# One-core convolution, attention and expert layer: each chunk's attention sums taken in two parts, and another order of loads at the end

## The chip, the cores and the metric

The kernel runs on one core of a Trainium2 chip: TensorE (PE, matrix products, and PEld, its weight loads), VectorE (DVE), ScalarE (ACT), GpSimd (POOL) and SyncE (SP), whose queue issues all the DMAs here. The metric is the device time of one execution in microseconds, the median of several runs.

## The reference, cut to what matters

Eight images of 128 channels and 36 x 36 = 1296 positions. Layer 0 is a convolution block with attention over 1156 positions and a residual. Layer 1 reads the result as 1296 tokens of 128 channels:

```python
t = _to_tokens(x)
t = t + _L1_attn_ref(_ln_t(t), ...)     # scores: sum_d w_d tanh(q_id + k_jd), softmax over j
t = t + _L1_ffn_ref(_ln_t(t), ...)      # 64 experts, each takes its 8 best tokens
x = _from_tokens(t, x)
```

```python
t = jnp.tanh(q[:, :, None, :] + k[:, None, :, :])
scores = jnp.einsum('bijd,d->bij', t, w) + bw[0]
attn = jax.nn.softmax(scores, axis=-1)
return jnp.einsum('bij,bjd->bid', attn, x)
```

In the expert layer each expert softmaxes its gate logits over the tokens, takes the weighted sum of its eight best tokens (`pooled`), passes it through two matrices with a gelu between, and adds its output back to those tokens with the same weights.

## The kernel before, in words

**The loop.** The work on the scores is divided into 8 batches (images) of 3 chunks of 432 queries, and each chunk goes through 11 tiles of keys: ten of 128 keys and a remainder of 16, which stands sixth in the list `order`. One tile of one chunk is a unit, and a unit takes 12 slots (3 for the remainder): 2952 slots in all. A slot is one turn of the main loop: TensorE makes two products for the denominators (`d`, three slots ahead) and two for the numerators (`n`), both at line L802 (L809 in the remainder unit); ScalarE takes Ln of `d` (L824) and, every second slot, Exp of two such (L827), which gives reciprocals; VectorE multiplies (L849, L855) and GpSimd and VectorE add up (L851, L862). Seven slots after a unit's last, its sum becomes the exponentials `e` of the scores (L887), a tile of 128 keys by 432 queries.

**Other work in the slots.** All the rest is written as generators in four lanes: `first_of_all` (query features of the next chunk), `urgent` (attend), `gates` (gating of the batch before) and `background` (layer 0, tokens and keys of the next batch). In each slot `take_turns` lets each lane take a step without matrix products, and `matmul_turn` lets one lane issue some, held by `PACE` to 370 units of work a slot on the average.

**Attend.** When all 11 `e` tiles of a chunk are there, `attend` goes to the urgent lane. For each of its four pieces of 108 queries (`TPC`) it issues the load of the piece's tokens into `t2` (L619), sums e times xh over the first six tiles into PSUM, copies this to `sums` (L632), sums the other five, adds (L634), divides and adds the tokens (L637), and takes statistics (L641, L642). Tiles `e` lie in a pool of NKT + 1 = 12. The gates lane takes no products while something is urgent. In the last batch, attend goes on to the gate logits of its chunk.

**The tail.** After the last slot the memory of the scoring pools is given back. SP issues, in this order: the expert biases (L1000, L1003), the first token tile of the last attend (`urgent.run`), the weights of four of 16 groups of experts (L992, L994, eight DMAs of 1 MB), then what `drain(*urgent)` issues: the other three token tiles (L619), t2d of the last chunk (L683) and, from `gate_tokens`, gd (L735). Then come eight loads of `gates` (L1025). The loop over the expert groups (inner L1033 and L1037, turned L1046, outer L1058) asks for the weights of one more group with each group that is done. After it: four stores of `out_s` to eod (L1077), eight loads of the residuals `res` from t2d (L1083) into a pool `lasts` of their own, four loads of `eo` (L1086) with an addition each (L1087), and for each batch three products (L1093) with three additions into `res` (L1094), followed by its store to the output (L1095).

All DMAs share eight completion semaphores in turn, so that a DMA waits until the one eight before it has landed. Pools rotate their buffers: a new tile waits for the readers of the one that had its buffer. `big` is a pool of eight tiles of 6 KB a partition, which the loop uses for images, weights of the convolutions, `xh`, `t2`, `probs`, `gt` and others.

Of the kernel before, what the change touches and what calls it, by code (L numbers as in the profile page):

```python
# [9 lines left out]
F32 = mybir.dt.float32  # L10
# [16 lines left out]
REM = KT[-1][1]  # L27
# [5 lines left out]
E, HID, O = 64, 512, 128  # L33
# [31 lines left out]
def kernel(  # L65
# [28 lines left out]
    nc = tc.nc  # L94
    mm = nc.tensor.matmul
# [25 lines left out]
    with ExitStack() as loop, ExitStack() as score:  # L121

        def pool(name, bufs, stack=loop, side="left", space=bass.MemoryType.SB):
            return stack.enter_context(
                tc.tile_pool(name=name, bufs=bufs, side=side, space=space)
            )


        big = pool("big", 8)
        chunks = pool("chunks", 14)  # L130
        etp = pool("etp", NKT + 1)
        one = pool("one", 1)
        two = pool("two", 2)
        kfp = pool("kfp", 3, score, "right")
# [9 lines left out]
        def big_tile(name):  # L144
            return big.tile([128, NT * 128], F32, tag="big", name=name)
# [4 lines left out]
        def aux(name):  # L150
            return ps_n.tile([128, 512], F32, tag="n", name=name)
# [4 lines left out]
        def load_x(b):  # L156
# [27 lines left out]
            out=gavg3, in_=gavg3, compare_op=ALU.is_ge, fill=0.0, base=0,  # L184
# [3 lines left out]
            out=gavg3, in_=gavg3, compare_op=ALU.is_ge, fill=0.0, base=C // G - 1,  # L188
# [46 lines left out]
        def bmm(out, lhsT, rhs, **kw):  # L235
            behind[0] += max(out.free_size(), 128) + 20
            mm(out, lhsT, rhs, **kw)  # L237
# [367 lines left out]

        attended = {}

        def attend(b, c, es):


            xh, _, xr = prepared[b]
            if c == 0:
                t2 = big_tile("t2").rearrange("p (t c) -> p t c", c=128)
                mv = two.tile([T, NT, 2], F32, tag="t2_mv", name="t2_mv")
                attended[b] = (t2, mv)
            t2, mv = attended[b]
            for i in range(TPC):
                at = c * TPC + i
                nc.sync.dma_start(t2[:T, at, :], tokd[b][at * T : (at + 1) * T])  # L619
                sums = two.tile([T, C + 1], F32, tag="sums", name="sums")  # L620
                for some in (range(6), range(6, NKT)):
                    pa = aux("pa1")[:T, : C + 1]
                    for j in some:
                        if j < NKT - 1:
                            e, v = es[j][:, i * T : (i + 1) * T], xh[:, j, :]
                        else:
                            rows = slice(32 * i, 32 * i + REM)
                            e, v = es[j][rows, :T], xr[rows]
                        bmm(pa, e, v, start=(j == some[0]), stop=(j == some[-1]))
                    yield TAKE  # L630
                    if j < NKT - 1:
# [5 lines left out]
                nc.vector.scalar_tensor_tensor(  # L637
                    t2[:T, at, :], pa[:, :C], inv, t2[:T, at, :], ALU.mult, ALU.add
                )
                st = small.tile([T, 6], F32, tag="t2_st", name="t2_st")  # L640
                nc.vector.bn_stats(st, t2[:T, at, :])  # L641
                nc.vector.bn_aggr(mv[:, at, :], st)  # L642
                yield matmuls()
            if c == NCH - 1:
                prepared.pop(b)
            if b == NB - 1:
# [120 lines left out]
        order = list(range(NKT - 1))  # L767
        order.insert(5, NKT - 1)
        units = [(b, c, j) for b in range(NB) for c in range(NCH) for j in order]
        slots = []  # L770
# [105 lines left out]
            nc.gpsimd.tensor_add(d, d, s[:, 0, T : 2 * T])  # L876
            return d

        es = {}

        def exps(p, u, d):
            b, c, j = units[u]

            while urgent and len(es.get((b, c), ())) == 1:
                urgent.run(p)
            e = etp.tile([128, CH], F32, tag="e", name="e")
            nc.scalar.activation(e[:, : d.shape[-1]], d, AF.Exp, bias=eb_s)  # L887
            es.setdefault((b, c), {})[j] = e
# [18 lines left out]
        first_of_all, urgent, gates, background = lanes = [Lane() for _ in range(4)]  # L907
        balance = [0]
# [29 lines left out]
        for u in range(2):  # L938
            prefetch(u)
        for p in range(LAG):  # L940
            denominators(p)
        pending = deque()
        for p, (u, k) in enumerate(slots):
            b, c, j = units[u]
# [44 lines left out]
        def load_experts(g):  # L989
            es = slice(g * EG, (g + 1) * EG)  # L990
            w1 = wts.tile([128, EG, HID], F32, tag="w1", name="w1")
            nc.sync.dma_start(w1, weight1[es, :128, :].rearrange("e d h -> d e h"))  # L992
# [19 lines left out]


    last = ctx.enter_context(tc.tile_pool(name="last", bufs=1))
    lasts = ctx.enter_context(tc.tile_pool(name="lasts", bufs=NB))

    def aux(name):
        return ps_last.tile([128, 512], F32, tag="aux", name=name)

    nc.vector.tensor_copy(pooled_s[:, :, NB - 1], pooled[:, :, NB - 1])  # L1020
    gates = []
    for h in range(NB // 2):
        gates.append(last.tile([128, N], F32, tag=f"gates{h}", name="gates"))
        for b in (2 * h, 2 * h + 1):
            nc.sync.dma_start(gates[h][E * (b % 2) : E * (b % 2) + E], gd[b])  # L1025

    out_s = last.tile([128, NGR, O], F32, tag="out_s", name="out_s")
    hidden, hidden_t, sums_of = {}, {}, {}
# [48 lines left out]
        nc.sync.dma_start(eods[q], out_s[32 * q : 32 * q + NB])  # L1077


    res, eos = [], []  # L1080
    for b in range(NB):
        res.append(lasts.tile([C, N], F32, tag="res", name="res"))
        nc.sync.dma_start(res[b], t2d[b])  # L1083
    for h in range(NB // 2):
        eos.append(last.tile([128, O], F32, tag=f"eo{h}", name="eo"))
        nc.sync.dma_start(eos[h], eod[2 * h : 2 * h + 2].rearrange("b e o -> (b e) o"))  # L1086
        nc.vector.tensor_add(eos[h], eos[h], b2_s)  # L1087
    for b in range(NB):
        half = slice(E * (b % 2), E * (b % 2) + E)
# [5 lines left out]
        nc.sync.dma_start(out[b], res[b])  # L1095


# [60 lines left out]
```

## Time and profile before

| | us |
|---|---|
| median of 3 runs (6334.52 to 6347.67) | 6334.6 |
| the profiled execution, as a run | 6322.6 |
| its span, first to last instruction | 6320.9 |
| Ln of the slots, first and last start | 182.1, 6128.4 |
| last exponential `e` ends | 6137.7 |
| last product of `ppool` ends | 6193.0 |
| `out_s` copied for the last time, from | 6276.5 |

The granted TensorE clock was 0.974 of full speed over the span; in the last 190 us it was at 0.50 to 0.60 in many stretches. "Busy" of an engine is the time in which it had an instruction running; for PE the ends are modelled. A wait in square brackets is idle time of the engine just before the instruction and what ended it. SPq is SP's queue: the duration of a DMA there is that of its issue, not of its transfer.

### The profile page before, as it was taken

To read this page: it belongs to the slowest core of one execution; us is meant where nothing else is said; L and a number is where in the kernel's file an instruction comes from. 1 tells how busy PE (TensorE), PEld (TensorE's weight loads), DVE (VectorE), ACT (ScalarE), POOL (GpSimd) and SP (SyncE) were. 2 spreads that over 40 slices of the span, in tenths; PEclk is the share of its full clock that TensorE was granted. 3 is DMA by queue.
4 is the path that set the end of the run, shared out by engine and by line. 5 is a ranking of instruction groups with operands and counts; after the bars stand their busy time and mean duration, and the time that the engine had idled before them with its cause. 6 is when DMAs were issued, how large, how long until landed. Compare 5 with 4: busy or idle time off the path is not lost.

```text
span 6320.9 us, 107144 instructions
## 1 busy us (share of the span) xinstructions
PE 6067.5 (96%) x40632; PEld 2825.9 (45%) x40632; DVE 4894.6 (77%) x9499; ACT 5360.3 (85%) x5426; POOL 4655.2 (74%) x2782
## 2 busy tenths in 40 slices
PE   8999999999999999999999999999999999999986
PEld 4444454444544444444444444444454444544433
DVE  3687778877788778887788787887778878778862
ACT  1788998888988889889888898888898988999970
POOL 3677777787778877778777786777777777778870
PEclk9999999999999999999999999999999999999997
DMA  0200011100210011100111001100021000100027
GB/s 27 71 30 22 23 64 37 31 24 27 68 36 20 29 35 58 34 27 22 51 44 36 22 23 59 42 30 25 23 69 36 23 25 27 59 28 28 25 69 256
DMA packets 155286, 265.81 MB, mean 42 GB/s; under 512 B 53712, under 2 KB 79824, under 8 KB 154768
## 3 DMA queue, kind: packets, MB, share of 16 engines
q1 hardware_dynamic: 154768, 258.95, 12.8%
q8 instruction: 319, 5.23, 0.4%
q14 instruction: 199, 1.63, 0.1%
HBM read 196.81 MB, written 61.83 MB: 41 GB/s over the span
## 4 chain that ended last, share of the span: by engine, by line
PE 68%; DVE 11%; ACT 8%; issue 7%; POOL 4%; DMA 1%; SPq 1%; POOLq 0%; DVEq 0%; ACTq 0%
PE n L802 31%; PE d L802 10%; PE pc L237 8%; PE pa L237 7%; ACT lq L824 5%; DVE n L849 3%; PE s L237 3%; DVE rp L855 3%; PE pk L237 2%; POOL accp L862 2%; DVE accd L851 2%; PE pq L237 1%; PE n L809 1%; PE d L809 1%; POOL qf L601 1%
## 5 line engine op out<-in xcount | busy, mean ns | idle before, releaser
L862 POOL TENSOR_TENSOR accp<-accp,rp 128x864 f32<-128x864 f32 x1464 | 2965.3, 2026 | 1137.6 <-DVE rp L855 1045.7
L802 PE MATMUL n<-qf,kf 32*128 32x432 f32 (+1 forms) x11520 | 3244.9, 575 | 54.4 <-DVE accd L851 10.0
L824 ACT ACTIVATE lq<-d 128x864 f32<-128x864 f32 x2952 | 2559.8, 883 | 587.2 <-PE d L802 515.1
L802 PE MATMUL d<-qf,kf 32*128 32x432 f32 (+1 forms) x11520 | 2889.0, 564 | 41.4 <-ACT lq L824 37.9
L855 DVE TENSOR_TENSOR rp<-n,lq 128x432 f32<-128x432 f32 x3984 | 2201.6, 600 | 565.5 <-PE d L802 374.4
L827 ACT ACTIVATE lq<-lq 128x1728 f32<-128x1728 f32 x1488 | 2431.1, 1634 | 47.1
L802 PEld LDWEIGHTS n<-qf,kf 32*128 32x128 f32 (+1 forms) x11520 | 1173.4, 185 | 1659.2 <-DVE rp L855 505.7
L802 PEld LDWEIGHTS d<-qf,kf 32*128 32x128 f32 (+1 forms) x11520 | 1036.0, 187 | 405.0 <-issue 236.0
L849 DVE TENSOR_TENSOR n<-n,lq 128x432 f32<-128x432 f32 x1440 | 812.0, 608 | 246.2 <-PE n L802 219.3
L851 DVE TENSOR_TENSOR accd<-n,accd 128x432 f32<-128x432 f32 x1440 | 867.9, 603 | 24.7
L860 POOL TENSOR_TENSOR accp<-rp 128x864 f32<-128x864 f32 x264 | 534.7, 2026 | 145.1 <-DVE rp L855 143.6
L869 POOL TENSOR_TENSOR accp<-accp 128x432 f32<-128x432 f32 x264 | 291.8, 1105 | 17.1
L237 PE MATMUL pa<-xh,e 128*108 128x129 f32 x1920 | 263.7, 284 | 30.4 <-DVE t L637 19.5
L237 PEld LDWEIGHTS pa<-xh,e 128*108 128x108 f32 x1920 | 224.3, 175 | 153.5 <-DVE rp L855 76.4
L872 POOL TENSOR_TENSOR accd<-accp,accd 128x432 f32<-128x432 f32 x240 | 266.0, 1108 | 34.8 <-DVE accd L851 17.2
L601 POOL TENSOR_SCALAR qf<-qf,cs_s 128x432 f32<-128x432 f32 x192 | 261.3, 1367 | 39.1 <-ACT qf L600 39.1
L237 PE MATMUL s<-q,k 128*116 128x432 f32 x480 | 228.8, 568 | 2.6 <-DVE q L260 2.1
L237 PEld LDWEIGHTS pk<-xT,a_k 128*128 128x128 f32 x1408 | 171.9, 193 | 108.6 <-issue 27.5
L381 ACT ACTIVATE e<-s 116x432 f32<-116x432 f32 x240 | 125.4, 522 | 109.7 <-PE s L237 108.6
L374 POOL TENSOR_TENSOR tot<-tot,e 116x432 f32<-116x432 f32 x192 | 212.6, 1107 | 5.1
L237 PE MATMUL pa<-e,vw 116*128 116x432 f32 x480 | 206.2, 556 | 3.9 <-DVE accd L851 3.0
L844 DVE TENSOR_TENSOR accd<-n,lq 128x432 f32<-128x432 f32 x240 | 144.8, 603 | 83.9 <-PE n L802 52.2
(180 smaller groups left out, 4025.0 us busy)
## 6 DMA issues: line engine op xcount, KB each, us to landing
kf<-kd SPq DMA_DIRECT2D x240, 512.0 KB
kd<-ks SPq DMA_DIRECT2D x160, 256.0 KB
w<-in_weight_dram SPq DMA_DIRECT2D x32, 1024.0 KB
x<-in_x_dram SPq DMA_DIRECT2D x8, 648.0 KB
t<-tokd SPq DMA_DIRECT2D x96, 54.0 KB
t2d<-t2T SPq DMA_DIRECT2D x24, 216.0 KB
res<-t2d SPq DMA_DIRECT2D x8, 648.0 KB
out_dram<-res SPq DMA_DIRECT2D x8, 648.0 KB
```

Source lines behind the costliest of these rows:

```text
L237: mm(out, lhsT, rhs, **kw)
L601: nc.gpsimd.tensor_scalar(qf[:, 1, :], qf[:, 0, :], cs_s[:, q : q + 1], None, ALU.mult)
L802: mm(outs[h][:, :CH], kf[rows[h], q, :], qf_of[b, c, q][rows[h], part, :], start=True, stop=True)
L824: nc.scalar.activation(lq[:, o : o + 2, :], d[:, :, :CH], AF.Ln)
L827: nc.scalar.activation(some, some, AF.Exp, scale=-1.0)
L849: mult(ns[h], ns[h], lq[:, o + h, :])
L851: nc.vector.tensor_add(live["d"], ns[h], live["d"])
L855: mult(rp[:, h, :], ns[h], lq[:, o + h, :])
L860: nc.gpsimd.tensor_add(live["p"], live["r"], rp)
L862: nc.gpsimd.tensor_add(live["p"], live["p"], rp)
L869: nc.gpsimd.tensor_add(s[:, 0, :], s[:, 0, :], s[:, 1, :])
L872: nc.gpsimd.tensor_add(d, s[:, 0, :], d)
```

## The change

Attend now enters the urgent lane when six of the chunk's eleven `e` tiles are there (`FIRST`). It first issues all four token loads, takes the first six tiles for all four pieces of queries and keeps the four sums in one tile `sums`; it then waits in its lane until the other five tiles are there, and finishes the four pieces. Tiles `e` lie in a pool of nine (`NES`), counted in `live_es`: when nine are taken, the urgent lane is run until some are given back. Gating waits until the batch's last attend is over (`whole`), and no longer stands back while something is urgent. At the end, SP's queue has the weights of four groups ahead of the biases, with the last token tiles loaded well before. The pool `big` outlives the loop, and the residuals are loaded into its eight buffers, each after one of the gate loads, ahead of the expert loop and of the fifth group's weights. The last products go in pairs, one for each batch of a pair, on the two halves of TensorE's rows; six additions are followed by two stores.

```diff
+FIRST = 6
+NES = 9
-        big = pool("big", 8)
+        big = pool("big", 8, ctx)
-        etp = pool("etp", NKT + 1)
+        etp = pool("etp", NES)
...
+            own = range(c * TPC, (c + 1) * TPC)
+            for at in own:
+                nc.sync.dma_start(t2[:T, at, :], tokd[b][at * T : (at + 1) * T])
+
+            def attended_to(i, some):
+                pa = aux("pa1")[:T, : C + 1]
+                for j in some:
...
+                    bmm(pa, e, v, start=(j == some[0]), stop=(j == some[-1]))
+                return pa
+
+            sums = one.tile([T, TPC, C + 1], F32, tag="sums", name="sums")
             for i in range(TPC):
-                at = c * TPC + i
-                nc.sync.dma_start(t2[:T, at, :], tokd[b][at * T : (at + 1) * T])
-                sums = two.tile([T, C + 1], F32, tag="sums", name="sums")
-                for some in (range(6), range(6, NKT)):
...
-                    yield TAKE
-                    if j < NKT - 1:
-                        nc.vector.tensor_copy(sums, pa)
-                        yield matmuls()
-                nc.vector.tensor_add(pa, pa, sums)
+                pa = attended_to(i, order[:FIRST])
+                yield TAKE
+                nc.vector.tensor_copy(sums[:, i, :], pa)
+                if i == TPC - 1:
+                    live_es[0] -= FIRST
+                yield matmuls()
+            while len(es) < NKT:
+                yield step()
+            yield matmuls()
+            for i, at in enumerate(own):
+                pa = attended_to(i, order[FIRST:])
+                yield TAKE
+                nc.vector.tensor_add(pa, pa, sums[:, i, :])
...
         def gating(b):
+            while b not in whole:
+                yield step()
...
-            while urgent and len(es.get((b, c), ())) == 1:
+            while live_es[0] == NES:
                 urgent.run(p)
...
-            if len(es[b, c]) == NKT:
-                urgent.append(attend(b, c, es.pop((b, c))))
+            if len(of_chunk) == FIRST:
+                urgent.append(attend(b, c, of_chunk))
...
-                    if lane is not first_of_all and balance[0] < 0 or lane is gates and urgent:
+                    if lane is not first_of_all and balance[0] < 0:
...
+        urgent.run(len(slots))
+        experts = [load_experts(g) for g in range(4)]
         b1_s = biases.tile([NGR, EG, HID], F32, tag="b1", name="b1_s")
...
-        urgent.run(len(slots))
-        experts = [load_experts(g) for g in range(4)]
...
-    gates = []
-    for h in range(NB // 2):
-        gates.append(last.tile([128, N], F32, tag=f"gates{h}", name="gates"))
-        for b in (2 * h, 2 * h + 1):
-            nc.sync.dma_start(gates[h][E * (b % 2) : E * (b % 2) + E], gd[b])
+    gates, res = [], []
+    for b in range(NB):
+        if b % 2 == 0:
+            gates.append(last.tile([128, N], F32, tag=f"gates{b}", name="gates"))
+        nc.sync.dma_start(gates[b // 2][E * (b % 2) : E * (b % 2) + E], gd[b])
+        res.append(big_tile("res")[:, :N])
+        nc.sync.dma_start(res[b], t2d[b])
...
-    res, eos = [], []
-    for b in range(NB):
-        res.append(lasts.tile([C, N], F32, tag="res", name="res"))
-        nc.sync.dma_start(res[b], t2d[b])
+    eos = []
...
+    for h in range(NB // 2):
         for c in range(NCH):
             cols = slice(c * CH, (c + 1) * CH)
-            pf = aux("pf")
-            mm(pf[:, :CH], eos[b // 2][half], gates[b // 2][half, cols], start=True, stop=True)
-            nc.vector.tensor_add(res[b][:, cols], pf[:, :CH], res[b][:, cols])
-        nc.sync.dma_start(out[b], res[b])
+            pfs = [aux("pf")[:, :CH] for _ in range(2)]
+            for i in range(2):
+                half = slice(E * i, E * i + E)
+                mm(pfs[i], eos[h][half], gates[h][half, cols], start=True, stop=True)
+            for i in range(2):
+                r = res[2 * h + i][:, cols]
+                nc.vector.tensor_add(r, pfs[i], r)
+        for b in (2 * h, 2 * h + 1):
+            nc.sync.dma_start(out[b], res[b])
```

More of the change, by code (lines that the diff above doesn't have):

```diff
@@ L606 @@
         attended = {}
+        whole = set()
         def attend(b, c, es):
@@ L616, in attend @@
             t2, mv = attended[b]
-            for i in range(TPC):
-                at = c * TPC + i
-                nc.sync.dma_start(t2[:T, at, :], tokd[b][at * T : (at + 1) * T])
-                sums = two.tile([T, C + 1], F32, tag="sums", name="sums")
-                for some in (range(6), range(6, NKT)):
-                    pa = aux("pa1")[:T, : C + 1]
-                    for j in some:
-                        if j < NKT - 1:
[L625 to L629, printed above, removed]
-                    yield TAKE
-                    if j < NKT - 1:
-                        nc.vector.tensor_copy(sums, pa)
-                        yield matmuls()
-                nc.vector.tensor_add(pa, pa, sums)
+            own = range(c * TPC, (c + 1) * TPC)
[4 more added lines that the diff above has]
+                for j in some:
+                    if j < NKT - 1:
+                        e, v = es[j][:, i * T : (i + 1) * T], xh[:, j, :]
+                    else:
+                        rows = slice(32 * i, 32 * i + REM)
+                        e, v = es[j][rows, :T], xr[rows]
+                    bmm(pa, e, v, start=(j == some[0]), stop=(j == some[-1]))
+                return pa
+            sums = one.tile([T, TPC, C + 1], F32, tag="sums", name="sums")
+            for i in range(TPC):
+                pa = attended_to(i, order[:FIRST])
[11 more added lines that the diff above has]
+                nc.vector.tensor_add(pa, pa, sums[:, i, :])
                 inv = small.tile([T, 1], F32, tag="inv", name="inv")
@@ L642, in attend @@
                 nc.vector.bn_aggr(mv[:, at, :], st)
+                if i == TPC - 1:
+                    live_es[0] -= NKT - FIRST
                 yield matmuls()
@@ L645, in attend @@
                 prepared.pop(b)
+                whole.add(b)
             if b == NB - 1:
@@ L877, in sums @@
             return d
-        es = {}
+        es, live_es = {}, [0]
         def exps(p, u, d):
             b, c, j = units[u]
-            while urgent and len(es.get((b, c), ())) == 1:
+            while live_es[0] == NES:
                 urgent.run(p)
             e = etp.tile([128, CH], F32, tag="e", name="e")
+            live_es[0] += 1
             nc.scalar.activation(e[:, : d.shape[-1]], d, AF.Exp, bias=eb_s)
-            es.setdefault((b, c), {})[j] = e
-            if len(es[b, c]) == NKT:
-                urgent.append(attend(b, c, es.pop((b, c))))
+            of_chunk = es.setdefault((b, c), {})
+            of_chunk[j] = e
+            if len(of_chunk) == FIRST:
+                urgent.append(attend(b, c, of_chunk))
         class Lane(deque):
@@ L1014 @@
     last = ctx.enter_context(tc.tile_pool(name="last", bufs=1))
-    lasts = ctx.enter_context(tc.tile_pool(name="lasts", bufs=NB))
     def aux(name):
@@ L1087 @@
         nc.vector.tensor_add(eos[h], eos[h], b2_s)
-    for b in range(NB):
-        half = slice(E * (b % 2), E * (b % 2) + E)
+    for h in range(NB // 2):
         for c in range(NCH):
             cols = slice(c * CH, (c + 1) * CH)
-            pf = aux("pf")
-            mm(pf[:, :CH], eos[b // 2][half], gates[b // 2][half, cols], start=True, stop=True)
-            nc.vector.tensor_add(res[b][:, cols], pf[:, :CH], res[b][:, cols])
-        nc.sync.dma_start(out[b], res[b])
+            pfs = [aux("pf")[:, :CH] for _ in range(2)]
[7 more added lines that the diff above has]
+            nc.sync.dma_start(out[b], res[b])
 def kernel(**inputs):
```

## The prediction, as it was made before the result

> **What bounds the kernel now.** I read the page first (engine busy times), then stretches of 20 and 5 us, then the timeline of the last 190 us with SP's queue on its own.
>
> ```profile
> PE 6067.5 (96%) x40632; PEld 2825.9 (45%) x40632; DVE 4894.6 (77%) x9499; ACT 5360.3 (85%) x5426; POOL 4655.2 (74%) x2782
> ```
>
> The span falls into a loop, to about 6138 us, and a tail of 183 us. In the loop TensorE is always occupied and ScalarE nearly so. I counted the 2952 Ln instructions (L824), one for each slot, in ScalarE's timeline: batches 1 to 6 take 750 to 758 us for 369 slots (2.04 us a slot), while the last batch, with no next batch to prepare, goes at ScalarE's pace. There the stretches (span of time, busy time of PE, PEld, DVE, ACT, POOL, granted clock, DMA share, GB/s) show what an attend costs:
>
> ```profile
> 5880.00:5900.00 20.00, 19.28 (x94) 7.34 (x94) 15.86 (x29) 19.81 (x22) 17.64 (x11) 1.00 0.09 26
> 5920.00:5940.00 20.00, 18.72 (x114) 9.56 (x112) 15.42 (x33) 18.43 (x17) 16.55 (x11) 1.00 0.01 2
> 5940.00:5960.00 20.00, 19.73 (x138) 11.46 (x134) 17.95 (x41) 16.79 (x16) 14.27 (x8) 1.00 0.11 33
> ```
>
> ACT is full at 19.81; the 44 products of one attend (about 5925 to 5956) take 1.38 + 3.02 = 4.4 us from it.
>
> The tail is where few things run at once. SP's queue:
>
> ```profile
> 6139.73 0.56 SPq L619 DMA_DIRECT2D t<-tokd  x1
> 6140.34 0.39 SPq L992 DMA_DIRECT2D w<-in_weight_dram  x1
> ...
> 6153.80 4.54 SPq L619 DMA_DIRECT2D t<-tokd  x3
> 6171.83 0.35 SPq L683 DMA_DIRECT2D t2d<-t2T  x1
> 6186.01 0.49 SPq L735 DMA_DIRECT2D gd<-gt  x1
> 6193.08 4.93 SPq L1025 DMA_DIRECT2D gates<-gd  x8
> 6198.11 0.54 SPq L992 DMA_DIRECT2D w<-in_weight_dram  x1
> ...
> 6277.18 3.76 SPq L1077 DMA_DIRECT2D eod<-out_s  x4
> 6280.98 6.95 SPq L1083 DMA_DIRECT2D res<-t2d  x8
> 6287.98 5.19 SPq L1086 DMA_DIRECT2D eo<-eod  x4
> 6305.37 11.31 SPq L1095 DMA_DIRECT2D out_dram<-res  x8
> ```
>
> and the waits that end last in it, from the timeline:
>
> ```profile
> 6166.47 0.35 DVE L637 SCALAR_TENSOR_TENSOR t<-pa,inv,t 108x128 f32<-108x128 f32 x1 [21.57 <-DMA t<-tokd]
> 6193.05 0.27 DVE L757 COPY pooled<-ppool 128x64 f32<-128x64 f32 x1 [4.84 <-PE ppool L237]
> 6270.78 1.07 PE L1033 MATMUL phid<-w,pooled_s 128*32 128x512 f32 x8 [1.68 <-DMA w<-in_weight_dram]
> 6299.60 0.90 DVE L1087 TENSOR_TENSOR eo<-eo,b_s 128x128 f32<-128x128 f32 x4 [22.46 <-DMA eo<-eod]
> ```
>
> The reader is to see three stalls: three token tiles queued behind eight weight transfers of 1 MB (DVE idle 21.57 us), the expert loop waiting for weights, and eo queued behind eight res (22.46 us). Stretches of 5 us tell when the DMA engines are full:
>
> ```profile
> 6155.00:6160.00 5.00, 0.00 (x0) 0.00 (x0) 0.00 (x0) 0.00 (x0) 0.00 (x0) 0.50 1.05 387
> 6175.00:6180.00 5.00, 1.70 (x2) 0.29 (x2) 1.54 (x5) 1.53 (x3) 0.00 (x0) 0.50 0.00 0
> 6200.00:6205.00 5.00, 5.00 (x49) 1.72 (x42) 0.06 (x1) 0.60 (x1) 0.00 (x0) 0.50 1.03 232
> 6265.00:6270.00 5.00, 3.74 (x52) 1.71 (x52) 0.69 (x1) 0.60 (x1) 0.00 (x0) 1.00 1.05 386
> ```
>
> Full at 386 GB/s in the weights, full at 232 GB/s in the gates (64 partitions), empty in between.
>
> **What the Trainium skill says.** "DMA: Bandwidth & Descriptors", section Specifications, puts HBM at about 358 GB/s a core; the trace has 386, and I use that. The same page, section Anatomy of one DMA, gives each DMA a fixed cost of about 2.0 us, mostly the receipt of the write, heaviest towards HBM; it is for GpSimd's path, and the trace only bounds it (the first t, alone at the front, was used 3.5 us after issue). "TensorE: Matmul & The Clock Gate", section What's actually happening, says that an idle window of about 3.4 us halves the clock and 3.4 us of activity restores it: the trace agrees in kind (0.50 through the tail's gaps). Its section on packing small matmuls lets different row groups run at once; the d and n products of 32 rows do so here.
>
> **The change part by part.** Times are of the profiled execution: span 6320.9, 6322.6 as a run; the median of the runs, 6334.6, is 12 us above, and I move the difference over.
>
> 1. Attend in two parts, in the loop. Products, copies and adds are the same in number (44 products a chunk, four copies, four adds), so TensorE's sum is unchanged. In the built program's order attend ran in slots 6 to 21 of the next chunk; now its first part runs in slots 69 to 77 of its own and the second in 7 to 13 of the next, with about 370 units of work a slot either way. Gating starts 8 slots earlier, layer 0 and the tokens of the next batch 9; the keys end where they did. Nine e buffers instead of twelve never hold anything up: a tenth exp comes 48 slots after the sixth, and the first part is over in some 10. I take 0 for 23 chunks, bounds +14 and -12, from the step that tells one batch from another now (750.5 against 757.6 us): two such steps.
> 2. The last chunk is different: its first 24 products used to run in the tail, beside the wait for tokens, and now run in the loop at ScalarE's pace. 24/44 of 4.4 us: +2.4 (bounds 0 and +4.4).
> 3. Tokens ahead. t is loaded in mid-loop, so the stall is gone. After the last exp (6137.8) 20 products are left, 40 instructions. The trace has x20 in 3.78 us while slow and x20 in 2.46 after: 6.2, at worst 7.6. The last L634 then comes at 6144.7 instead of 6169.65: -25. Everything to ppool (L691, gate softmax, max, transposes) follows unchanged in 23.4 us, ending at 6168 instead of 6193. The eight weight transfers now go first, at about 6133 (they need only the last products and multiplications, not the last exp as b1 did), and land by 6159: 7 us of early start, worth nothing, since the gates wait for ppool. b1 and b2 behind them are needed at 6168 only: 0.
> 4. Residuals in the loop's buffers. Eight res (5.31 MB) now stand between gates and the fifth group's weights. SP takes them in order, the gates wait for ppool, so 2.65 + 5.31 MB pass before the 25.17 MB of weights. Before, the stream from 6193 to 6270.8 carried 27.8 MB; it now starts 25 us earlier with 5.31 MB more. Those cost 13.8 us at 386 GB/s if nothing overlaps, 9.4 if they fill what the gates leave idle (11.2 us at 237 GB/s leave 1.7 MB): I take 11.5. The last group starts 25 - 11.5 = 13.5 us earlier (bounds 11 and 16).
> 5. eo without res ahead of it. From the last eod issue (ends 6280.94) to the eo addition 18.7 us pass. What stays is the landing of eod, four issues and the landing of eo: 5.5 us with the page's 2.0 twice and 1.5 of issues, 8.5 with 3.5 twice. I take 7: -11.7 (bounds -10 and -13).
> 6. The end. Products in pairs of row halves, 24 additions of 0.53 us as before, but the first out waits for six additions instead of three, and two outs go at the end. Before, first out at 6305.37 and end at 6320.9: 15.5 us for 5.3 MB, so the outs bound this stage. Pairs save about two slow products of 1.45 us, the three more additions cost 1.6 and two last outs 1.7: +0.5 (bounds -1 and +2).
>
> Sum: +2.4 - 13.5 - 11.7 + 0.5 = -22.3: 6300.3 as a profiled run, 6334.6 - 22.3 = 6312 as a median.
>
> **Rivals.** A: slower. The statistics of the next batch's tokens (11 pairs on DVE, 5 us) and its tanh with two table loads (3.9 us on ACT) each stop TensorE once a batch and slow its clock. They move from slots 310-312 and 298 to 301-303 and 289, so the statistics now fall on the remainder unit (its d products at 303-305, n at 306-308), which is all TensorE work. Where the clock was low over such a unit (5562 to 5590 us) eight slots took 27.7 us instead of 16. At 8 to 12 us a batch, four of seven batches are the point from which it decides: -22 + 4 x 9 = +14; with all seven about 6375. Against it: the tanh moves off that unit, and DVE has only two multiplications a slot in it. B: the loop gains. Gating's two activations and its max and replace leave slots 52 to 58, just ahead of the other remainder unit (60-62): 3 us in each of seven batches (the nine slots from 54 on take 20 us where nine usual ones take 17 to 18), -22 - 21 = -43: 6291. Against it: part of those 20 us is the unit's own work. C: the gain is mostly given back: the res cost all of 13.8 us, eod and eo 8.5, the end +2, the last chunk +4.4, the loop +7 (one step as in 1): -11.2 - 10.2 + 2 + 4.4 + 7 = -8: 6327. For it speaks that the DMA engines are full for most of the tail in any order; against it, that each term has to fall on its bad side.
>
> **Chances.** Forecast 0.62, A 0.09, B 0.14, C 0.15. The forecast's own range, with the bounds of 1 to 6 not all on one side, is 6299 to 6324; to leave out no more than 2 in 10 I go to 6291 (B) and 6330 (beyond C). No change from a change is told apart at 0.2%, 12.7 us: faster 0.62 x 0.98 + 0.14 = 0.75 and a share of C, 0.77; same 0.14; slower 0.09.
>
> **What would show it.** Right: no DVE wait for t at the end, ppool's copy near 6170, the last w about 11 us earlier, eo 25 us earlier, res among the weights at 386 GB/s, batches of 750 to 758 us. Wrong: DMA gaps after ppool, gates before it (then step 4 costs less), or batches longer by more than 3 us with slow products in the remainder unit (A).

## The result, and the profile after

The changed kernel is slower: median 6420.19 us of 4 runs (6412.33 to 6421.84) against 6336.38 us of the kernel before (now of 4 runs; the prediction had 6334.6 of 3), a ratio of 1.0126 (95% interval 1.0109 to 1.0144). The forecast was 6312 us. The profiled execution took 6420.13 us, its span 6418.4 us, at a mean granted clock of 0.962 (before 0.974).

Two points of the traces part the span: the start of the last Ln (before 6128.4, after 6244.8 us) and the end of the last exponential e (6137.7 and 6254.1 us). The loop is 116.4 us longer, the tail from the last e to the end 18.9 us shorter (183.2 to 164.3 us). So the tail won most of what was forecast (24.7 us), and the loop, which was put at nothing, lost six times as much as the tail won. (By the profiled executions the change costs 97.5 us, by the medians 83.8: the profiled one of before lies 14 us below its median, so the loop's loss against a usual run is nearer 102 us.)

The page's line of busy times of the changed kernel (us, share of the span, instructions):

```profile
PE 6133.3 (96%) x40632; PEld 2878.1 (45%) x40632; DVE 4888.1 (76%) x9499; ACT 5358.5 (83%) x5426; POOL 4651.7 (72%) x2782
```

The counts of PE, VectorE, ScalarE and GpSimd are those of before, and the busy times of the last three are within 7 us of it. Only TensorE is busy for longer, PE by 66 us with the same 40632 instructions: they ran slower. The loss is in waiting and in the clock, not in work.

The waits of the changed kernel from 160 to 6240 us (engine and line, what it waited for; us in total, times, longest):

```profile
PE pa L239 <- ACT e L909: 58.9, 39, 2.9
PE d L823 <- ACT lq L845: 35.8, 70, 3.0
...
ACT lq L845 <- PE d L823: 620.1, 702, 7.8
```

and those of the kernel before, with the one place of its wait of `pa` on `e` in the timeline:

```profile
PE d L802 <- ACT lq L824: 37.9, 63, 4.1
PE pa L237 <- ACT e L887: 2.4, 1, 2.4
...
ACT lq L824 <- PE d L802: 515.1, 675, 4.6
...
6137.79 0.47 PE L237 MATMUL pa<-xh,e 128*108 128x129 f32 x2 [2.39 <-ACT e L887]
```

A wait is new: the attend products `pa` stop TensorE until an exponential is there, 58.9 us in 39 places. Before, the only such place comes after the loop, at the very last exponential; every kernel below has that one too. In the loop there was none. And ScalarE waits 105 us more for the next `d`. The timeline of the changed kernel shows how one leads to the other, in the first part of a chunk of the fourth batch (start, duration, what ran; in brackets the idle time before and its releaser):

```profile
2873.63 1.36 PE L239 MATMUL pa<-xh,e 128*108 128x129 f32 x10 [0.25 <-DVE accd L872]
...
2875.25 1.64 ACT L848 ACTIVATE lq<-lq 128x1728 f32<-128x1728 f32 x1
...
2876.80 0.37 ACT L909 ACTIVATE e<-accp,eb_s 128x108 f32<-128x108 f32 x1
...
2877.22 0.36 PE L239 MATMUL pa<-xr,e 16*108 16x129 f32 x1 [2.24 <-ACT e L909]
...
2878.35 1.79 PE L823 MATMUL n<-qf,kf 64*128 64x432 f32 x4
2878.47 0.89 ACT L845 ACTIVATE lq<-d 128x864 f32<-128x864 f32 x1 [1.30 <-PE d L823]
...
2881.62 0.89 ACT L845 ACTIVATE lq<-d 128x864 f32<-128x864 f32 x1 [2.26 <-PE d L823]
```

The first part begins in the very slot in which the sixth exponential, the remainder's, is issued. Its first five products (ten instructions, for the trace has two to a product) read old tiles and pass; the sixth reads the new one, which stands on ScalarE behind Ln and an Exp of 1.64 us. TensorE stops for 2.24 us with the products of the next slots queued behind. Those (2877.23 and later) come only after it: "The MATMULs themselves stay in program order", says the Trainium skill ("TensorE: Matmul & The Clock Gate", section Step-by-step: what each phase is for), and the trace agrees. Now ScalarE has used up the `d` tiles that were ready and starves in its turn, 1.30 and then 2.26 us. Stretches of 4 us of the same place (busy time of PE, PEld, DVE, ACT, POOL, granted clock, DMA share, GB/s):

```profile
2870.00:2874.00 4.00, 3.75 (x27) 1.47 (x24) 3.56 (x7) 3.97 (x5) 3.44 (x2) 1.00 0.00 0
2874.00:2878.00 4.00, 1.76 (x19) 1.28 (x18) 1.52 (x4) 3.14 (x4) 2.21 (x2) 1.00 0.00 0
2878.00:2882.00 4.00, 4.00 (x16) 1.67 (x12) 2.87 (x7) 1.27 (x2) 2.01 (x1) 0.57 0.00 0
2882.00:2886.00 4.00, 4.00 (x34) 2.68 (x33) 2.77 (x6) 3.94 (x5) 0.70 (x1) 1.00 0.00 0
```

After the stop the clock is at 0.57 for the next 4 us, four instructions of n take 1.79 us instead of the 1.00 of four a little earlier (at 2870.72), and ScalarE is busy for 1.27 of 4 us: two engines with 96 and 83% of the span stop one after the other. Summed in such stretches from the first Ln to the last, TensorE's idle time went from 138 to 192 us, and the time lost to the clock, (1 - clock) x length, from 105 to 184 us.

Every batch is longer, counted from the start of its first Ln to that of the next batch's (of the last one, to its last Ln): the first seven by 7 to 19 us, and the last, which has no next batch to prepare, by most, 24.5 us (668.2 to 692.7).

In the tail, the steps went as follows. SP's queue of the changed kernel:

```profile
6141.43 1.63 SPq L623 DMA_DIRECT2D t<-tokd  x4
6249.62 0.39 SPq L1015 DMA_DIRECT2D w<-in_weight_dram  x1
...
6282.69 0.45 SPq L1047 DMA_DIRECT2D gates<-gd  x1
6283.19 0.58 SPq L1049 DMA_DIRECT2D res<-t2d  x1
...
6387.84 3.80 SPq L1101 DMA_DIRECT2D eod<-out_s  x4
6395.33 1.76 SPq L1107 DMA_DIRECT2D eo<-eod  x4
6402.65 10.34 SPq L1121 DMA_DIRECT2D out_dram<-res  x8
```

Its timeline, at the places of the three stalls of before:

```profile
6259.90 0.27 DVE L650 TENSOR_TENSOR pa<-pa,sums 108x129 f32<-108x129 f32 x1
6282.70 0.27 DVE L778 COPY pooled<-ppool 128x64 f32<-128x64 f32 x1 [4.83 <-PE ppool L239]
6397.29 0.60 DVE L1108 TENSOR_TENSOR eo<-eo,b_s 128x128 f32<-128x128 f32 x2 [9.48 <-DMA eo<-eod]
```

and stretches of 5 us:

```profile
6290.00:6295.00 5.00, 5.00 (x46) 2.08 (x43) 0.00 (x0) 0.60 (x1) 0.00 (x0) 0.50 1.04 301
6295.00:6300.00 5.00, 5.00 (x35) 1.29 (x38) 0.69 (x1) 0.51 (x1) 0.00 (x0) 0.50 1.02 264
...
6365.00:6370.00 5.00, 4.57 (x61) 2.08 (x54) 1.38 (x2) 0.60 (x1) 0.00 (x0) 0.82 1.04 387
...
6380.00:6385.00 5.00, 4.33 (x44) 2.11 (x36) 0.63 (x1) 0.60 (x1) 0.00 (x0) 0.50 0.02 3
```

Counted from the end of the last e: the last addition of attend comes at +5.8 instead of +31.9 us, ppool's copy at +28.6 instead of +55.3, the first store to eod at +133.7 instead of +139.4, and from the end of the eod issues to the addition on eo 5.7 us pass instead of 18.7. The reader is to see that DVE's wait for t is gone, that gates and residuals fill the DMA engines at only 264 to 301 GB/s where weights move at 387, and that after the weights are in, the last groups still work up to the first store at 6387.84 us, at a clock of 0.50 and with the DMA engines all but empty (share 0.02).

### The profile page after: what moved, and what is told of

It is laid out like the page before. It is cut to its first block, busy times and chain, and to the rows that moved or that the text cites. A ratio compares the mean times of both kernels' runs of the same rounds, so it can differ in the third digit from the quotient of the medians.

```text
span 6418.4 us, 107170 instructions
## 1 busy us (share of the span) xinstructions
PE 6133.3 (96%) x40632; PEld 2878.1 (45%) x40632; DVE 4888.1 (76%) x9499; ACT 5358.5 (83%) x5426; POOL 4651.7 (72%) x2782
## 4 chain that ended last, share of the span: by engine, by line
PE 69%; DVE 12%; ACT 8%; issue 7%; POOL 2%; DMA 1%; SPq 1%; DVEq 0%; POOLq 0%; ACTq 0%
PE n L823 31%; PE d L823 11%; PE pc L239 7%; ACT lq L845 6%; PE pa L239 5%; DVE n L870 3%; PE s L239 3%; DVE rp L876 3%; PE pk L239 3%; PE pq L239 2%; DVE accd L872 2%; PE n L830 1%; PE d L830 1%; ACT e L909 1%; ACT lq L848 1%
## 5 line engine op out<-in xcount | busy, mean ns | idle before, releaser
L823 PE MATMUL n<-qf,kf 32*128 32x432 f32 (+1 forms) x11520 | 3254.9, 579 | 46.8 <-DVE accd L872 13.8
L823 PEld LDWEIGHTS d<-qf,kf 32*128 32x128 f32 (+1 forms) x11520 | 1054.1, 188 | 391.8 <-issue 227.5
```

The costliest lines, as they stand in the source:

```text
L823: mm(outs[h][:, :CH], kf[rows[h], q, :], qf_of[b, c, q][rows[h], part, :], start=True, stop=True)
```

## The experiments

Two theories. **N** (newest exponential): the loss is the stop of TensorE before products that read an exponential just issued, with the slow clock and the starved ScalarE behind it. **S** (shift): the loss comes from where the next batch's preparation now falls against the remainder's unit, as in the forecast's rival A. "Wait" below is the wait of pa on e as in the view above, but only up to the last exponential, so without the one that every kernel has behind the loop; idle and clock are TensorE's idle time and the time lost to the clock, summed as above; all of one profiled execution each. The medians come from 4 to 20 runs, with the kernel before timed beside them (6336 to 6341 us).

| kernel | median us | ratio, 95% interval | wait us (times) | idle | clock |
|---|---|---|---|---|---|
| before | 6336.38 | 1 | 0 | 138 | 105 |
| after | 6420.19 | 1.0126 (1.0109 to 1.0144) | 58.9 (39) | 192 | 184 |
| e1 tail alone | 6318.45 | 0.9968 (0.9953 to 0.9983) | 0 | 139 | 119 |
| e2 both parts late | 6325.47 | 0.9973 (0.9960 to 0.9986) | 0 | 115 | 132 |
| e3 remainder seventh | 6366.41 | 1.0044 (1.0028 to 1.0060) | 27.1 (28) | 187 | 106 |
| e4 e2 and e3 | 6338.73 | 1.0004 (0.9994 to 1.0014) | 0 | 143 | 89 |
| e5 first part late | 6323.75 | 0.9974 (0.9964 to 0.9984) | 12.3 (15) | 143 | 132 |
| e6 e2 and norm earlier | 6279.59 | 0.9914 (0.9895 to 0.9932) | 0 | 125 | 95 |
| e7 e1, newest first | 6420.75 | 1.0128 (1.0109 to 1.0147) | 53.2 (23) | 192 | 165 |
| e8 e1, residuals split | 6299.69 | 0.9946 (0.9926 to 0.9965) | 0 | 141 | 122 |
| e9 second part late | 6362.34 | 1.0048 (1.0029 to 1.0067) | 28.7 (18) | 148 | 147 |
| e10 norm earlier | 6387.59 | 1.0081 (1.0063 to 1.0099) | 54.5 (42) | 174 | 131 |
| e11 e1, norm earlier | 6336.40 | 1.0004 (0.9996 to 1.0013) | 0 | 142 | 110 |
| e12 e6, residuals split | 6271.37 | 0.9904 (0.9889 to 0.9919) | 0 | 127 | 100 |

**e1, the tail alone.** The loop of before, with the four token loads at the start of attend and all of the change's tail:

```diff
+            for at in range(c * TPC, (c + 1) * TPC):
+                nc.sync.dma_start(t2[:T, at, :], tokd[b][at * T : (at + 1) * T])
             for i in range(TPC):
                 at = c * TPC + i
-                nc.sync.dma_start(t2[:T, at, :], tokd[b][at * T : (at + 1) * T])
```

> The loop of the kernel before with the tail of the changed one (weights ahead of biases, residuals in the loop's buffers among the gates, products in pairs), and the four token loads of a chunk at the start of its attend. Attend itself is in one piece after the eleventh exponential. If the loss is all in the loop (both theories below): loop as before within 8 us (last Ln of the slots near 6128), tail 16 to 19 us shorter, 6317 to 6321 as a median. If instead the tail's residuals or the buffers kept beyond the loop cost something: no faster than before, 6336 or more.

6318.45 us, 19 us faster than the kernel before that was timed beside it: what the tail gains comes out as time once the loop is left alone. The last Ln, expected within 8 us of 6128, starts at 6142.8 us; that is about the 14 us by which the profiled execution of before was a quick one. From this loop to that of the change (last exponential at 6152.2 and 6254.1 us) it is 102 us, as between the medians. The loss is in the two parts.

**e2, both parts late.** Two steps of the loop pass before a first part's products, one more before a second's:

```diff
+            yield step(2)
+            yield matmuls()
             sums = one.tile([T, TPC, C + 1], F32, tag="sums", name="sums")
...
             while len(es) < NKT:
                 yield step()
+            yield step(1)
             yield matmuls()
```

> The changed kernel with the products of the first part two slots later and those of the second one slot later, so that the exponential that was issued last is done when TensorE comes to it. Theory N (TensorE stops at the first products of each part for the newest exponential, 58.9 us in 39 waits, and what follows from the stop): the waits of pa on e fall below 10 us and the time by 60 to 100 us, to 6320 to 6360. Theory S (the tokens' statistics and the tanh of the next batch now fall on the remainder unit): they stay where they are (slots 302 to 304), so the time falls by no more than 15 us, 6405 or more.

6325.47 us: the loss in the loop is gone but for 7 us against e1, which the runs' spread covers. The exponential and its readers in the trace of e2, same chunk as above:

```profile
2848.45 0.37 ACT L912 ACTIVATE e<-accp,eb_s 128x108 f32<-128x108 f32 x1
...
2851.93 1.36 PE L239 MATMUL pa<-xh,e 128*108 128x129 f32 x10
...
2853.22 0.36 PE L239 MATMUL pa<-xr,e 16*108 16x129 f32 x1
```

and its stretches there:

```profile
2846.00:2850.00 4.00, 4.00 (x18) 1.72 (x20) 3.18 (x6) 3.57 (x4) 2.52 (x3) 1.00 0.00 0
2850.00:2854.00 4.00, 3.87 (x34) 2.13 (x30) 3.55 (x7) 3.06 (x3) 2.11 (x2) 1.00 0.00 0
2854.00:2858.00 4.00, 3.73 (x27) 1.73 (x23) 3.43 (x8) 3.67 (x5) 3.81 (x3) 1.00 0.41 131
```

The reader comes 4.4 us after its exponential instead of at once; there is no stop, TensorE stays at 1.00, and ScalarE is busy for 3.06 to 3.67 of each 4 us.

**e3 and e4, the remainder in the seventh place**, in the changed kernel (e3) and in e2 (e4):

```diff
-        order.insert(5, NKT - 1)
+        order.insert(6, NKT - 1)
```

> The changed kernel with the remainder unit seventh in the order of key tiles, not sixth: its slots go from 306 to 308 to 318 to 320, away from the tokens' statistics (301 to 303) and the transposes that wait for them. Theory S: 5 to 8 us less in each of seven batches, 6365 to 6385. Theory N: the waits of pa on e stay, as the sixth exponential is still used at once (now that of a whole tile): 6405 to 6425.

> Parts later and the remainder unit seventh. Whichever theory holds, the gains add up: with N about 80 and S about 40, below 6316, which is the kernel before less its tail's gain; if a third cause holds the larger part of the loop's 116 us, the time stays above 6360.

e3 gains 54 us and lands where S put it, but it is no clean test of S: the first part's newest exponential is another tile's, and the wait itself fell from 58.9 to 27.1 us. The gains of e2 and e3 don't add, as e4's expectation had it (below 6316): with the waits gone the same move costs 13 us. So nothing of the loss is left for S where the waits are gone. The last batch says the same: S can't act in it, and it lost the most.

**e5 and e9, one part late at a time.** e5 has only the first two added lines of e2, e9 only the third.

> The changed kernel with one edit: two steps of the loop are let pass before the products of a chunk's first part, nothing before those of its second. In the changed kernel's trace TensorE stands still before products that read the exponential just queued on ScalarE: 47.0 us in 24 first parts (each waits, for the remainder's exponential), 11.9 us in 15 second parts. Theory N (this stop, and the clock and the starving of ScalarE behind it, is the loss): four fifths of the 95 us that both delays together won come back, so about 6345 us (6330 to 6360); the waits of pa on e fall to 12 us or less. Rival (the second part, at the chunk's end, meets the next chunk's start and is what costs): under a third comes back, 6390 or more.

> The changed kernel with one more step let pass before the products of a chunk's second part and nothing else: the edit that the expectation of the run e6 speaks of. (The kernel of e6 was another: both delays, and besides two steps less between the group norm's variance and its reciprocal root in the preparation of the next batch. Its trace has no wait of pa on e left, and it took 6279.59 us.) Theory N, by the waits: the first parts alone hold 47 of 59 us of waits, and the run with only the first part delayed (6323.75 us) won all that both delays won, so here 47 us of waits stay and nearly all of the loss: 6400 us or more, the gain between 0 and 20 us. Rival (any one of the two delays moves the rest of the loop's work off a bad place): under 6360.

e5 wins back all 96 us, although 15 waits are left in the second parts. e9 wins 58 us, far more than the 20 that N by the waits allowed and near the rival's figure; but it does so with fewer waits than expected: in its trace the first parts keep 28.7 us, not 47. That moving the second part also moves the first part that comes after it is a likely reason, not a shown one. By the waits that are left these runs do line up: 58.9 us at 6420, 28.7 at 6362 (and e3's 27.1 at 6366), 12.3 at 6324, none at 6325. The last 12 us cost nothing that can be seen, so it isn't one price for each microsecond, and the two edits' gains don't add.

**e7, the newest first in the loop of before.** e1 with the two groups of tiles exchanged:

```diff
-                for some in (range(6), range(6, NKT)):
+                for some in (range(6, NKT), range(6)):
...
-                    if j < NKT - 1:
+                    if some[0] == 6:
                         nc.vector.tensor_copy(sums, pa)
```

> No two parts here: the kernel before with the tail of the change (as the run of the tail alone, 6318.45 us), and one edit in how a chunk is attended to: of a token tile's two groups of products the one over tiles 6 to 10 goes ahead of the one over tiles 0 to 5, so that the products first given to TensorE read the exponential issued last. Same instructions, same count. Theory N: TensorE waits for that exponential as in the second parts of the changed kernel (0.5 to 1.4 us at a chunk, some 12 us in all), and at the rate seen so far (95 us for 59 us of waits) 15 to 25 us are lost: 6333 to 6345 us. Rival (the wait is a symptom, what costs is that the work lies in two places of a chunk, in the slots where other lanes are due): no change beyond 6310 to 6327 us.

6420.75 us: 102 us slower than e1. That is far more than either expectation, because the wait is: 53.2 us in 23 chunks, not 12 us (the view's 57.7 in 24 has the one behind the loop, 4.5). Its waits, one of the places in its timeline and the stretch that follows:

```profile
PE pa L237 <- ACT e L888: 57.7, 24, 4.5
```

```profile
3002.56 0.64 ACT L888 ACTIVATE e<-accd,eb_s 128x432 f32<-128x432 f32 x1
...
3003.25 0.47 PE L237 MATMUL pa<-xh,e 128*108 128x129 f32 x2 [2.44 <-ACT e L888]
...
3005.19 0.89 ACT L825 ACTIVATE lq<-d 128x864 f32<-128x864 f32 x1 [1.99 <-PE d L803]
```

```profile
3004.00:3008.00 4.00, 4.00 (x18) 1.33 (x10) 2.44 (x5) 0.89 (x1) 1.89 (x1) 0.57 0.00 0
```

The same stop, the same slow clock and the same starving of ScalarE behind it, in a kernel with no two parts, with the same instructions as e1. The order in which one chunk's products read their tiles is enough to make a loss as large as the whole.

**e6, e10, e11: the norm earlier.** e6 was meant to be what e9 is; the kernel that ran had both delays of e2, and this besides, in the preparation of the next batch:

```diff
             ve = plus_eps(pv[:, :1], 1e-5, [C, 1])
-            yield step(2)
             rs = small.tile([C, 1], F32, tag="gn_rs", name="gn_rs")
```

Its expectation is for the other edit and says nothing of this one:

> The changed kernel with one edit: one more step of the loop is let pass before the products of a chunk's second part, nothing before those of its first. Theory N: a fifth of the 95 us comes back, about 6400 us (6385 to 6412), with some 47 us of waits of pa on e left, all in first parts. Rival (the second part is what costs): 6360 or less. If the two single edits together win much less or much more than both at once did, the waits do not add, and one of them covers the other.

It took 6279.59 us, 46 us less than e2. e10 has the edit alone in the changed kernel, e11 in e1:

> The changed kernel, its two parts where the change puts them, with one edit in the preparation of the next batch: the two steps between the group norm's variance and its reciprocal root are left out, so that all that the lane does after it comes two slots earlier in each batch. In the run e6 this came on top of both delays and was worth 46 us there (6325.47 to 6279.59). Theory N alone: the waits of pa on e stay near 59 us and the time at 6400 us or more. Theory S (the place of the preparation's later stages against the key remainder's unit is a cost of its own, which the change made worse): the clock's deficit in slots 288 to 323 of a batch falls and the time comes to 6365 to 6390. If it is below 6340, the waits are not the cause of the loss.

> The run of the tail alone (loop of the kernel before, 6318.45 us) with the same two steps left out of the next batch's preparation. In the loop of before the stages after the group norm stand elsewhere against the remainder's unit. If the two steps are worth something by themselves, whatever the loop (less to wait for): 6265 to 6290. Theory S (a matter of what meets what in the slots): anything from 6295 to 6345, not the same 46 us; the wait of TensorE on xh in the remainder's unit grows or shrinks with it.

e10 gains 33 us, as S had it, with the waits nearly as they were (54.5 us), while the time lost to the clock falls from 184 to 131 us; e11 loses 18. So the place of the preparation in the slots is worth tens of microseconds by itself, in either sign: that much of S holds. How it acts isn't shown. e11's expectation tied it to the wait on xh; that wait (n at L803 there, L801 in e11) fell from 8.3 to 3.2 us while the time rose.

Six pairs of runs differ in the delays, or in e7's order, and so in the waits of pa on e, and have the rest alike. The trace's record of the granted clock tells what followed each stop. It knows two values, 1.00 and 0.50; "slow clock" is half the length of the spells at 0.50 that begin during a stop or within 2 us of its end.

| with the waits, without | stops, us | slow clock, us | both | difference of the medians, us |
|---|---|---|---|---|
| after, e2 | 58.9 | 34.1 | 93.0 | 94.7 |
| e7, e1 | 53.2 | 54.6 | 107.8 | 102.3 |
| e3, e4 | 27.1 | 3.4 | 30.5 | 27.7 |
| e9, e2 | 28.7 | 23.9 | 52.6 | 36.9 |
| e5, e2 | 12.3 | 0 | 12.3 | -1.7 |
| e10, e6 | 54.5 | 8.5 | 63.0 | 108.0 |

The medians are good to some 10 us. In the first three pairs the stops and the slow clock right behind them make up the loss to within 6 us. Where few slow spells follow, as in e3, a microsecond of stop costs about one; where most stops bring one, it costs nearly two. In e9 and e5 the loss is some 15 us less than the two together, and in e10 it is 45 us more: there something else costs time, and what it is stays open.

**e8 and e12, residuals split.** Four residual loads go behind the last weights, four behind the loads of eo, in e1 (e8) and in e6 (e12):

```diff
         res.append(big_tile("res")[:, :N])
-        nc.sync.dma_start(res[b], t2d[b])
...
             experts.append(load_experts(len(experts)))
+            if len(experts) == NGR:
+                for b in range(NB // 2):
+                    nc.sync.dma_start(res[b], t2d[b])
...
         nc.vector.tensor_add(eos[h], eos[h], b2_s)
+    for b in range(NB // 2, NB):
+        nc.sync.dma_start(res[b], t2d[b])
```

> The run of the tail alone (6318.45 us) with one edit: the eight residual loads no longer stand ahead of the weights of the last groups; four stand behind the last weights and ahead of the stores of the experts' sums, four behind the loads of eo. It tells how large the prediction's step 4 is by itself: there the residuals' 5.3 MB were put at 13.5 us of the weight stream, while the trace of the change has gates and residuals together at 257 to 301 GB/s, which puts the residuals' share at 18 to 21 us. If the stream is what the tail waits for, the first store of the sums comes 13 to 21 us earlier after the last exponential (137.7 us in the tail-alone trace), the add on eo follows within 6 to 9 us of the last of them, the end comes up to 5 us later after that add than the 21 us of now: 6302 to 6314 us, a version ahead of both kernels. Rival (the last groups' own work, at a low TensorE clock, is what the tail waits for): the store comes less than 8 us earlier and the time stays at 6313 or more.

> The kernel of e6 (both parts late, the two steps of the group norm left out; 6279.59 us) with the residual loads split about the stores of the experts' sums as in e8, which won 18.8 us over the tail alone and 16.7 us at the first store. The loop is not touched, so the gains add: 6258 to 6268 us, ahead of every kernel so far. If it is 6275 or more, the two do not add.

SP's queue at the end of e8:

```profile
6262.07 4.50 SPq L1078 DMA_DIRECT2D res<-t2d  x4
6277.32 3.81 SPq L1081 DMA_DIRECT2D eod<-out_s  x4
6284.78 1.75 SPq L1087 DMA_DIRECT2D eo<-eod  x4
6286.58 2.93 SPq L1090 DMA_DIRECT2D res<-t2d  x4
```

The last e ends at 6156.3 us, so the first store comes at +121.0 us; in e1 it came at +137.7. Without the residuals ahead of the weights it came 16.7 us earlier. The first four now load while the last groups compute, a time in which the changed kernel's DMA engines were empty. From the addition on eo to the end 23.7 us pass instead of 21.2. e8 gains 18.8 us on e1. e12 gains 8 us on e6 by the medians, where 12 to 22 were expected; but its tail, from the last exponential to the end, is 17.4 us shorter in the trace (146.7 after 164.1), against 14.2 in e8, and its loop, the same code, happened to run 5 us longer. The runs of e6 spread over 24 us and those of e12 over 11, so the medians of four don't tell 8 from 19. e12, 6271.37 us, is the fastest: 1.0% ahead of the kernel before and 2.3% ahead of the change.

## Why the prediction was wrong

**Step 1, attend in two parts, is the step that failed.** It took 0 with bounds of +14 and -12 us; the loop of the profiled execution became 116.4 us longer. The counts of products, copies and adds in it are right, and so are the nine e buffers: the exponentials on ScalarE (L909) wait once in the whole run, for 6.2 us and for GpSimd's sum, as they did before. What it left out is what the products wait for. The forecast knew from the built order that the first part starts at slot 69 of its chunk, and that a tile's exponential comes seven slots after its unit; those are one and the same slot, and `order[:FIRST]` reads that tile. Before, each piece read the tiles in the order of their numbers, so that the newest, tile 9, came in the second group, a turn of the lane behind six old ones. So the step counted the products and left out their wait: 58.9 us of stops, and 34.1 us of slow clock right behind them, together 93 of the 95 us that e2 wins back. The bound came from the spread of batches in the kernel before (751.0 to 757.6 us for the second to the seventh, when the starts of the Ln are counted again), in whose loop the wait doesn't occur, so it couldn't hold it. e7 shows the cause by making it, e2 by taking it away, and e5 by taking it out of the first parts alone.

**Rival A** had the sign but not the mechanism: its chance was 0.09 and its time at most 6375 us. Its collision can be seen (n of the remainder on xh at L548, 14.2 us in 5 places, in the waits of the changed kernel), and e10 shows that shifts matter by 33 us. But e2 wins the loss back without any edit of the preparation, and the last batch, which prepares nothing, is the one that lost most (24.5 us, with 9.6 us of stops and 8.5 of slow clock behind them). Rivals B and C had the loop 21 us shorter and 7 us longer; neither came.

**Step 2**, +2.4 us for the last chunk's products in the loop, can't be told apart in a last batch that is 24.5 us longer; in e2, without the waits, the last batch is 6.5 us longer than before and 3.9 longer than in e1, and e5 and e6 have it shorter than either.

**Step 3** was right: the last addition comes 26.1 us earlier (25), ppool's copy 26.7 us earlier, with no wait for t.

**Step 4** was mis-sized: 13.5 us (11 to 16) for the last group, and the first store came 5.7 us earlier. The last place at which both kernels wait for weights is the group before the last:

```profile
6265.35 1.06 PE L1033 MATMUL phid<-w,pooled_s 128*32 128x512 f32 x8 [1.66 <-DMA w<-in_weight_dram]
6372.20 1.06 PE L1057 MATMUL phid<-w,pooled_s 128*32 128x512 f32 x8 [1.65 <-DMA w<-in_weight_dram]
```

Counted from the last e it comes 9.5 us earlier (127.6 to 118.1), so 17.2 of the 26.7 us from step 3 are lost by then (put at 11.5, at most 13.8; e8's 16.7 fits): gates and residuals, interleaved, move at 264 to 301 GB/s and not at 386. The lower bound of 9.4 let the residuals fill what the gates leave idle, but the prediction's own stretch of the gates has the DMA engines at a share of 1.03 with 232 GB/s: nothing was idle. Another 3.8 us are lost from there to the first store, 15.6 us instead of 11.8: from 6375 us on the clock is at 0.50, where before it was at 1.00 and then 0.82. This second term was not in the sum.

**Step 5** was right: eod to eo takes 5.7 us instead of 18.7, a gain of 13.0 (11.7). **Step 6**: from the addition on eo to the end 21.1 instead of 21.3 us (+0.5).

## What to carry to other kernels

When work is moved to an earlier place, look not only at what it costs and where it stands, but at how old its newest operand is at that place: on an engine that works through its queue in order, a product that reads what another engine has just been asked for holds up everything behind it, and the engine it feeds next. Read the oldest operands first and let a few steps of the loop pass before the newest; here two steps before the first part were worth 96 us. Of a transfer that is moved ahead of a saturated stream, take the rate of that kind of transfer, not of the stream, and count no gap in which the engines' share is already full.

## What the runs showed of the hardware

Stops far shorter than expected can bring the slow clock. The Trainium skill ("TensorE: Matmul & The Clock Gate", section What's actually happening) puts the window at about 3.4 us idle; here one stop of 2.24 us, in 4 us with 1.76 us of work, was followed by 4 us at 0.57. Over the 165 waits of pa on e in the loops of the six kernels that have them, a spell at 0.50 followed 38 of the 40 stops of 2.2 us and more (the longest 3.2), 8 of the 20 between 1.6 and 2.1, 2 of the 33 between 1.0 and 1.6 and none of the 72 shorter ones; each spell took 3.41 or 6.83 us. So the length of a stop doesn't decide alone.

The same section has about 3.4 us of activity restore the clock. In the tail of the changed kernel the trace differs: between 6290 and 6300 us PE was busy for 10 of 10 us at 0.50 throughout. The ends of products are modelled in it, so some of this time may have been idle; what counts as activity isn't shown.
